# A two-layer decoder kernel: order of early loads, a product split over chunks, and passes moved between engines

## Chip, cores and metric

The kernel runs on one core of one Trainium2 chip. Its time is the device time of one execution in microseconds, as a median over runs. A second execution is recorded by the hardware profiler, and all durations below come from that record. The core has a matrix engine (TensorE, PE), three engines for elementwise work (VectorE or DVE, ScalarE or ACT, GpSimd or POOL) and a queue engine (SyncE or SP). DMA transfers are issued from the instruction streams of SP, ACT and POOL. PEld is the load of a stationary operand, which overlaps with PE.

## What is computed

Two layers work on `x` of shape (2, 512, 1024) with a context of shape (2, 1024, 1024), all in float32:

```python
x = x + fake_quant(layernorm(x)) @ fake_quant(ctx)            # layer 0, first part
x = x + layer_0_ffn(layernorm(x))                             # W, b, and routed low-rank terms
x = x + attention(layernorm(x), ctx, ctx, mask, wq, wk, wv, wo)   # layer 1: 32 heads, 8 key heads, rope
x = x + layer_1_ffn(layernorm(x))                             # W_up and a gated low-rank term

def fake_quant(x, scale, zp):
    q = clip(round(x / scale + zp), 0, 255)
    return (q - zp) * scale

# routing in layer_0_ffn: one softmax for each batch from the mean of some rows
q = x[:, 179:-1, :].mean(axis=1)
routing = softmax(q @ router_W.T + router_b)                  # 8 experts
```

The gate of the last part takes the best of four experts for each token.

## The kernel before

**Products.** Each large product is done by a scheme with seven block products instead of eight. A left matrix and a right matrix are cut into quarters, sums of quarters are made (`left_steps`, `right_steps`: four sums each), and seven products of sums are accumulated in 128x512 PSUM banks (`seven`, in the order 1, 2, 6, 7, 5, 4, 3). Products 1 and 2 need only raw quarters, the others need sums. A generator yields after each block product. `pair(a, b)` alternates two such generators for two products each and then runs them one after the other; `weave` advances a side generator between the yields of a main one. There are four PSUM tiles with the tag "b", each one bank, and two of the tag "wide", each two banks. SBUF tiles come from four groups of buffers: u8 (14), u4 (17), u2 (10) and small (16).

**Order.** TensorE's order is the order of the program text everywhere. VectorE's and ScalarE's order is the program's in two places, inside the blocks that say so: the first stage, and all of attention up to its last steps, where GpSimd's is too. Elsewhere a planner, which works from modelled costs when the kernel is built, orders VectorE, ScalarE, GpSimd and the queues. SP's queue is always ordered by the planner. Each engine and each queue then runs strictly in that order, so one that waits holds back all behind it.

**Start.** The first stage computes keys of batch 0 in rotated form (`keys`, `rope_steps`). L1043 to L1046 load the first key weight quarter on SP and the first context quarter on ScalarE's queue in four chunks each; L1047 to L1062 load the rest in order of need. Eight small constants (quantizer scales and zero points, router bias and weights, gate bias and weights) are loaded by GpSimd's queue at the top (L119, L139 to L146), and VectorE derives six more from them (L123 to L133).

**Layer 0, first part.** `quantized_product` is a side generator. It loads eight 128x1024 rows of the context for each batch, quantizes them with three VectorE passes each (L194, L197, L198), does the same with four normalized rows of `x`, turns those by TensorE (L431, copied out by L156) and multiplies. `copy_out`, L284 (first copy in `seven`), L216 and L217 (the halves of the rope rotation) and L434 run on ScalarE. Meanwhile the main stream does the remaining keys and then the values. `quad_weights` (L370) issues four weight loads on SP and makes their sums; it is called after each stage's `weave`.

**Router.** `routed` makes the mean row (`qm`) on VectorE, then eight f32 products of 128x128 with 128x8 on TensorE (L630), and the softmax.

**Queries and the seam into attention.** `queries` makes query heads four at a time for q = 0 to 7. A rope is done in two steps: the two ScalarE copies (L216, L217), and then three elementwise passes (L219 on VectorE, L222 and L223 on the engine given). For q = 7 the second step is put into the list `later`, on GpSimd; `rotate` in attention runs it. Attention runs from step n = -2 on; head n+2 is new, n+1 is in the middle, n is old. Each step has three phases: scores of the new head (L768, with the mask added by L782 on VectorE); a tree of maxima (L790 to L796) with products of other stages in between, whose number for q = 7 is in `extra`; then maximum and sum over partitions (L732, L734), written to a row in DRAM (L741) and read back broadcast (L747), the copy of the maximum into a PSUM bank (`place_maximum`, L810), two halves of the exponential (L814 on VectorE, L817 on ScalarE, sums L820 to L825 on GpSimd), and the product with the values (`attend`, L831, copied out by L839). L842 normalizes on GpSimd in the next step.

**Gates.** Near the end, `gated` is advanced by hooks at (step, phase): products with the gate weights (L967, copied out by L975), transposes (L981), a chain of small VectorE passes (L982 to L996), transposes back (L1005). `projection` (`seven_onto`, first copy L320) and `linear` are the products around it.

Of the kernel before, what the change touches and what calls it, by code (L numbers as in the profile page):

```python
# [18 lines left out]
P = 128  # L19
# [20 lines left out]
def decoder_kernel(  # L40
# [67 lines left out]
    eps_t = const.tile([P, 1], F32, name="eps_t")  # L108
    nc.gpsimd.memset(eps_t, EPS)
    prefer = const.tile([P, E1], F32, name="prefer")  # L110
# [6 lines left out]
    for name, ap in qparams.items():  # L117
        t = const.tile([P, 1], F32, name=f"qp_{name}")
        nc.gpsimd.dma_start(t, ap.partition_broadcast(P))  # L119
        qp[name] = t  # L120
    for side in ("x1", "x2"):
        t = const.tile([P, 1], F32, name=f"qp_inv_{side}")
        nc.vector.reciprocal(t, qp[f"{side}_scale"])  # L123
        qp[f"{side}_inv"] = t
# [3 lines left out]
    for c_t, side in ((c_x1, "x1"), (c_x2, "x2")):  # L128
        nc.vector.tensor_scalar(c_t, qp[f"{side}_zp"], -1.0, QMID, ALU.mult, ALU.add)
    kc2 = const.tile([P, 1], F32, name="kc2")  # L130
    nc.vector.tensor_scalar_mul(kc2, c_x2, float(D))
    s12 = const.tile([P, 1], F32, name="s12")
    nc.vector.tensor_tensor(s12, qp["x1_scale"], qp["x2_scale"], ALU.mult)  # L133
# [5 lines left out]
    nc.gpsimd.dma_start(rb_t, rb0.partition_broadcast(P))  # L139
    eb_t = const.tile([P, E1], F32, name="eb_t")  # L140
    nc.gpsimd.dma_start(eb_t, ebias.partition_broadcast(P))
    r0_t = const.tile([P, NC, E0], F32, name="r0_t")
    nc.gpsimd.dma_start(r0_t, r0T.rearrange("(c p) e -> p c e", p=P))
    NGA = E1 + E1 * R1
    ga_t = const.tile([P, NC, NGA], F32, name="ga_t")
    nc.gpsimd.dma_start(ga_t, gaT.rearrange("(c p) e -> p c e", p=P))  # L146
# [45 lines left out]
    def quantized(dst, src, side):  # L192

        nc.vector.tensor_scalar(  # L194
            src, src, qp[f"{side}_inv"], qp[f"{side}_zp"], ALU.mult, ALU.add
        )
        nc.vector.tensor_scalar(src, src, 0.0, QMAX, ALU.max, ALU.min)  # L197
        nc.vector.tensor_scalar(dst, src, RND, RND + QMID, ALU.add, ALU.subtract)  # L198
# [71 lines left out]
    def seven(product, emit):  # L270
# [5 lines left out]
        for i in (1, 2, 6, 7, 5, 4, 3):  # L276
            first = {2: 1, 4: 7, 3: 5}.get(i, i)
            if i == first:
                banks[i] = ps_b()
            acc = banks[first]  # L280
            product(i, acc, i == first)
# [82 lines left out]
    def quad_weights(dram, q):  # L364

        raw = []
        for mh in range(2):
            for ch in range(2):
                w = u4([P, 4, 256])
                nc.sync.dma_start(w, dram[q, mh, ch])  # L370
                raw.append(w)
        return quad_sums(raw)
# [109 lines left out]
    def keys(b, q, ctx_ops, w):  # L482
        def group(m):
            def product(i, acc, start):
                accumulate(
                    acc,
                    [(w[i - 1][:, c, ts(m, P)], ctx_ops[i - 1][:, c, :]) for c in range(4)],
                    start,
                )

            def emit(i, j, src):
                dst = u2([P, HALF]) if (i, j) == (0, 0) else src
                rope(dst, src, j, 1.0)
                nc.sync.dma_start(kT_d[b][4 * q + 2 * i + m][:, ts(j, HALF)], dst)

            return seven(product, emit)

        return group(0), group(1)
# [110 lines left out]
    def routed(b, quarters, a_t, b_t, result):  # L609
# [15 lines left out]
        nc.vector.tensor_scalar_mul(qm[:, 0, :], qm[:, 0, :], 1.0 / (Q_END - Q_START))  # L625
        yield
        yield
        racc = ps_b()
        for c in range(NC):
            nc.tensor.matmul(  # L630
                racc[:, :E0],
                qm[:, 0, c : c + 1].to_broadcast([P, P]),
                r0_t[:, c, :],
                start=(c == 0),
                stop=(c == NC - 1),
            )
# [31 lines left out]
    def queries(q, h_ops, w, later=None):  # L668

        def head(m):  # L670
# [7 lines left out]
            def finish(i, j, src):  # L678
                dst = u2([P, HALF]) if (i, j) == (0, 0) else src
                eng = nc.vector if later is None else nc.gpsimd  # L680
# [175 lines left out]
    def attention(extra):  # L856
# [28 lines left out]
        for n in range(-2, total + GRP + 1):  # L885
# [36 lines left out]
            for _ in range(extra.pop(n, 0)):  # L922
                for _ in range(2):
                    next(tree, None)
                next(extra["products"])
            if n == GRP:
# [5 lines left out]
            if mid:  # L932
                mid.place_maximum()
# [109 lines left out]
    for c in range(4):  # L1043
        cs = slice(c, c + 1)
# [31 lines left out]
    with tc.manual_schedule(engines={mybir.EngineType.DVE, mybir.EngineType.Activation}):  # L1076
# [3 lines left out]
        advance(lefts, 2)  # L1080
        for g in first[0]:
# [17 lines left out]

    side = layer_0()  # L1100
    for b in range(B):
# [5 lines left out]
        for i, stage in enumerate((keys, keys, values, values)):  # L1107
# [57 lines left out]
    early = [head for q in range(2) for head in queries(q, h_ops, w[q])]  # L1165
# [9 lines left out]
    for q in range(NH // 4):  # L1175
        heads = (
            early[2 * q : 2 * q + 2]
            if q < 2
            else queries(q, h_ops, w, later if q == NH // 4 - 1 else None)
        )  # L1180
# [3 lines left out]
        if q < NH // 4 - 1:  # L1184
            for _ in main:
                pass
# [5 lines left out]
    extra = {-2: 3, -1: 3, 0: 2, 1: 2, 2: 2, 3: 1, 4: 1}  # L1192
# [40 lines left out]
    for i in range(2):  # L1233
# [11 lines left out]
    hooks[(62, 1)] = [lambda: advance(last["gates"], 3)]  # L1245
    hooks[(62, 2)] = [
        lambda: fetch_weight(7, 0, 1),
        lambda: fetch_weight(3, 1, 1),
    ]
    with tc.manual_schedule(  # L1250
# [6 lines left out]
        for i in range(3 * (B * NH + 2)):  # L1257
# [4 lines left out]
            if (n - 2, phase) == (63, 1):  # L1262
                zT = next(last["gates"])
# [6 lines left out]
                advance(main, 2)  # L1270

# [123 lines left out]
```

## Time and profile before

| what | us |
|---|---|
| median of 3 runs (lowest to highest) | 2451.58 (2450.2 to 2452.53) |
| the profiled execution | 2450.07 |
| its span, first to last instruction | 2448.3 |
| TensorE busy in the span | 2412.5 |
| first key product waits, last chunk used from | 13.74 |
| first value product begins | 114.26 |
| attention begins, first scores | 929.97 |
| last matmuls | from 2416.90 |

The span is what the instructions of the kernel cover; the execution has 1.8 us more around it. In all views, times count from the first instruction. A row of a timeline has the start, the time that the merged instructions took, engine, line, operation, the tile written and those read, the shape, how many they are, and in brackets the idle time before them with what ended it. The page also cuts the span into 40 equal slices; these two lines give the busy share of TensorE and of the DMA engines in each, in tenths:

```profile
PE   8999999999999999999999999999999999999999
...
DMA  5537133013796221244323323442433343233501
```

TensorE is full nearly everywhere. The DMA engines are full only around 650 to 750 us, and half used at the start.

### The profile page before, as it was taken

To read this page: it belongs to the slowest core of one execution; us is meant where nothing else is said; L and a number is where in the kernel's file an instruction comes from. 1 tells how busy PE (TensorE), PEld (TensorE's weight loads), DVE (VectorE), ACT (ScalarE), POOL (GpSimd) and SP (SyncE) were. 2 spreads that over 40 slices of the span, in tenths; PEclk is the share of its full clock that TensorE was granted. 3 is DMA by queue.
4 is the path that set the end of the run, shared out by engine and by line. 5 is a ranking of instruction groups with operands and counts; after the bars stand their busy time and mean duration, and the time that the engine had idled before them with its cause. 6 is when DMAs were issued, how large, how long until landed. Compare 5 with 4: busy or idle time off the path is not lost.

```text
span 2448.3 us, 19583 instructions
## 1 busy us (share of the span) xinstructions
PE 2412.5 (99%) x6792; PEld 1195.8 (49%) x6800; DVE 1841.1 (75%) x1994; ACT 530.8 (22%) x623; POOL 1031.3 (42%) x550
## 2 busy tenths in 40 slices
PE   8999999999999999999999999999999999999999
PEld 3477458654444443444444444444444444444444
DVE  4949774345876556898888888888898998888653
ACT  1210221011222222322222222222222222222210
POOL 0000010210000001677676767667776767677621
PEclk9999999999999999999999999999999999999999
DMA  5537133013796221244323323442433343233501
GB/s 182 181 105 273 69 134 108 26 60 116 274 330 216 78 91 56 77 156 111 81 83 107 114 65 90 142 145 79 125 116 79 94 125 112 66 90 108 172 9 60
DMA packets 149010, 288.01 MB, mean 118 GB/s; under 512 B 29424, under 2 KB 47360, under 8 KB 146608
## 3 DMA queue, kind: packets, MB, share of 16 engines
q1 hardware_dynamic: 108080, 244.35, 29.9%
q10 hardware_dynamic: 40400, 41.70, 6.9%
q8 instruction: 54, 0.88, 0.2%
q0 software_dynamic: 432, 0.71, 0.1%
q14 instruction: 44, 0.36, 0.1%
HBM read 223.54 MB, written 63.18 MB: 117 GB/s over the span
## 4 chain that ended last, share of the span: by engine, by line
PE 60%; DVE 6%; POOL 2%; issue 1%; DMA 1%; ACT 1%; ACTq 0%; SPq 0%; DVEq 0%; POOLq 0%
PE b L355 26%; PE wide L768 16%; PE b L831 15%; PE wide L732 2%; DVE u L814 2%; DMA u<-in_wo_dram 1%; DVE u L782 1%; POOL u L823 0%; POOL u L824 0%; DVE small L734 0%; DVE u L792 0%; DVE u L794 0%; ACT u L817 0%; POOL u L825 0%; DVE u L328 0%
## 5 line engine op out<-in xcount | busy, mean ns | idle before, releaser
L355 PE MATMUL b<-u,u 128*128 128x512 f32 (+1 forms) x3616 | 1394.2, 542 | 21.3 <-DMA u<-in_ctxT_in_dram 7.6
L355 PEld LDWEIGHTS b<-u,u 128*128 128x128 f32 x3616 | 684.6, 191 | 695.9 <-issue 612.8
L768 PE MATMUL wide<-u,u 128*128 128x512 f32 x1024 | 454.8, 595 | 7.3 <-DVE u L782 6.4
L831 PE MATMUL b<-u,u 128*128 128x512 f32 x1024 | 460.3, 592 | 0.0
L782 DVE TENSOR_TENSOR u<-wide,u 128x1024 f32<-128x1024 f32 x256 | 312.8, 1224 | 130.3 <-PE wide L768 129.9
L817 ACT ACTIVATE u<-u 128x2048 f32<-128x2048 f32 x128 | 244.7, 1912 | 655.8 <-DVE u L814 593.9
L768 PEld LDWEIGHTS wide<-u,u 128*128 128x128 f32 x1024 | 193.4, 190 | 257.3 <-issue 177.9
L814 DVE TENSOR_TENSOR u<-u,b 128x2048 f32<-128x2048 f32 x128 | 290.2, 2268 | 0.0
L820 POOL TENSOR_TENSOR u<-u 128x1024 f32<-128x1024 f32 x64 | 151.5, 2367 | 317.5 <-ACT u L817 310.1
L831 PEld LDWEIGHTS b<-u,u 128*128 128x128 f32 x1024 | 186.2, 192 | 184.6 <-issue 184.6
L310 POOL TENSOR_TENSOR u<-u,u 128x512 f32<-128x512 f32 x120 | 188.5, 1597 | 175.4 <-DVE u L322 153.2
L328 DVE TENSOR_TENSOR u<-u,b 128x512 f32<-128x512 f32 x200 | 135.8, 680 | 126.0 <-PE b L355 125.9
L222 POOL TENSOR_TENSOR u<-u,sin_t 128x512 f32<-128x512 f32 x8 | 11.6, 1456 | 402.7 <-ACT u L217 402.7
L823 POOL TENSOR_TENSOR u<-u,u 128x1024 f32<-128x1024 f32 x64 | 150.7, 2354 | 36.4 <-ACT u L817 36.0
L824 POOL TENSOR_TENSOR u<-u,u 128x1024 f32<-128x1024 f32 x64 | 150.8, 2356 | 5.0
L842 POOL TENSOR_TENSOR u<-u,u 128x512 f32<-128x512 f32 x64 | 119.9, 1873 | 10.0 <-DMA u<-row 10.0
L216 ACT ACTIVATE u<-u 64x512 f32<-64x512 f32 x72 | 45.2, 628 | 356.3 <-DVE u L293 177.6
L790 DVE TENSOR_TENSOR u<-u 128x1024 f32<-128x1024 f32 x64 | 115.8, 1810 | 0.0
L732 PEld LDWEIGHTS wide<-ident,u 128*128 128x128 f32 x512 | 79.6, 203 | 63.9 <-issue 55.0
L612 POOL TENSOR_TENSOR u<-u,u 128x1024 f32<-128x1024 f32 x8 | 20.2, 2529 | 214.9 <-DVE u L168 111.6
L792 DVE TENSOR_TENSOR u<-u,u 128x1024 f32<-128x1024 f32 x64 | 105.4, 1646 | 0.2
L825 POOL TENSOR_TENSOR u<-u 128x512 f32<-128x512 f32 x64 | 101.0, 1578 | 5.0
(135 smaller groups left out, 1614.3 us busy)
## 6 DMA issues: line engine op xcount, KB each, us to landing
u<-row ACTq DMA_DIRECT2D x128, 256.0 KB, 3.7
u<-wo SPq DMA_DIRECT2D x64, 512.0 KB, 4.0
u<-in_wo_dram SPq DMA_DIRECT2D x48, 512.0 KB, 4.5
u<-in_wq_dram SPq DMA_DIRECT2D x32, 512.0 KB, 4.2
q<-u SPq DMA_DIRECT2D x64, 256.0 KB, 2.4
u<-in_wo_dram SPq DMA_DIRECT2D x16, 1024.0 KB, 8.2
wo<-u SPq DMA_DIRECT2D x32, 512.0 KB, 4.2
u<-q SPq DMA_DIRECT2D x64, 256.0 KB, 4.2
```

Of the source, the lines that this page charges most:

```text
L310: nc.gpsimd.tensor_tensor(c, c, what, ALU.add)
L328: nc.vector.tensor_tensor(c, c, acc, ALU.add)
L355: nc.tensor.matmul(acc, lhsT, rhs, start=start and k == 0, stop=k == len(pairs) - 1, skip_group_check=True,)
L732: nc.tensor.transpose(tr[:, t, :], src[:, t, :], ident)
L768: nc.tensor.matmul(sc[:, ts(n, HALF)], self.kT[:, ts(2 * j + n, P)], self.qT, start=True, stop=True,)
L782: nc.vector.tensor_tensor(self.e[j // 2][:, js, :], sc.rearrange("p (k q) -> p k q", k=2), mask[j], ALU.add)
L814: nc.vector.tensor_tensor(e, e, self.nmf.unsqueeze(1).to_broadcast([P, 4, S]), ALU.add)
L817: nc.scalar.activation(e, e, AF.Exp)
L820: nc.gpsimd.tensor_tensor(d, e[:, 0:2, :], e[:, 2:4, :], ALU.add)
L823: nc.gpsimd.tensor_tensor(d, d, e[:, 0:2, :], ALU.add)
L824: nc.gpsimd.tensor_tensor(d, d, e[:, 2:4, :], ALU.add)
L831: nc.tensor.matmul(self.acc, self.v[:, k, :], self.e[j][:, k % 4, :], start=(k == 0), stop=(k == NKT - 1),)
```

## The change

Eight edits, in the order of the program:

1. The eight small loads leave GpSimd's queue and come on SP behind the last weight of the first stage. The constants made from them come after the first stage.
2. The first pass of the quantizer (`x * inv + zp`) runs on ScalarE instead of VectorE, 24 passes in all.
3. The first quarter products of keys 0 and 1 are computed together, chunk by chunk, into two banks (`begun`) that `seven` then takes as product 1. The loads come in three chunks, of one, one and two 128-row blocks. Twenty 128x128 bf16 products on a tile of ones come ahead of them.
4. The raw value weights for the first value stage are requested before the weave of the second key stage instead of after it; the sums of them stay after it.
5. The router's eight products become an elementwise product and a sum on VectorE, and one product with ones.
6. `queries` takes its rope engine as an argument; q = 6 also defers its second rope step by one yield, and its last one goes into attention. The steps -2 and -1 of attention do 2 and 4 products instead of 3 and 3, and in step -1 the maximum and both exponentials stand between these products.
7. In every later step the read of the sum's row (`old.den`) comes after the second exponential instead of before the new maximum.
8. The third step of the gates comes after attention of its step, and the last one after the first two products of `linear`.

```diff
@@ constants
-    eps_t = const.tile([P, 1], F32, name="eps_t")
+    eps_one = const.tile([P, 2], F32, name="eps_one")
+    eps_t, one_t = eps_one[:, 0:1], eps_one[:, 1:2]
     nc.gpsimd.memset(eps_t, EPS)
+    nc.gpsimd.memset(one_t, 1.0)
...
-    for name, ap in qparams.items():
-        t = const.tile([P, 1], F32, name=f"qp_{name}")
-        nc.gpsimd.dma_start(t, ap.partition_broadcast(P))
-        qp[name] = t
-    for side in ("x1", "x2"):
-        t = const.tile([P, 1], F32, name=f"qp_inv_{side}")
-        nc.vector.reciprocal(t, qp[f"{side}_scale"])
-        qp[f"{side}_inv"] = t
+    for name in list(qparams) + ["x1_inv", "x2_inv"]:
+        qp[name] = const.tile([P, 1], F32, name=f"qp_{name}")
...
@@ def quantized(dst, src, side):
-        nc.vector.tensor_scalar(
-            src, src, qp[f"{side}_inv"], qp[f"{side}_zp"], ALU.mult, ALU.add
+        nc.scalar.activation(
+            src, src, AF.Identity, bias=qp[f"{side}_zp"], scale=qp[f"{side}_inv"]
         )
@@ def seven(product, emit, begun=None):
-                banks[i] = ps_b()
+                banks[i] = begun if begun is not None and i == 1 else ps_b()
             acc = banks[first]
-            product(i, acc, i == first)
+            if begun is None or i > 1:
+                product(i, acc, i == first)
@@ def quad_weights(dram, q):
+        return quad_sums(raw_weights(dram, q))
+
+    def raw_weights(dram, q):
         raw = []
...
-        return quad_sums(raw)
+        return raw
@@ def routed(b, quarters, a_t, b_t, result):
+        weighted, each = u2([P, E0, NC]), small([P, E0])
+        nc.vector.tensor_tensor(
+            weighted,
+            r0_t.rearrange("p c e -> p e c"),
+            qm[:, 0, :].unsqueeze(1).to_broadcast([P, E0, NC]),
+            ALU.mult,
+        )
+        nc.vector.tensor_reduce(each, weighted, AX.X, ALU.add)
         yield
         yield
         racc = ps_b()
-        for c in range(NC):
-            nc.tensor.matmul(
-                racc[:, :E0],
-                qm[:, 0, c : c + 1].to_broadcast([P, P]),
-                r0_t[:, c, :],
-                start=(c == 0),
-                stop=(c == NC - 1),
-            )
+        nc.tensor.matmul(
+            racc[:, :E0], one_t.to_broadcast([P, P]), each, start=True, stop=True
+        )
@@ def queries(q, h_ops, w, eng, later=None):
-                eng = nc.vector if later is None else nc.gpsimd
@@ attention, phase 2
-            for _ in range(extra.pop(n, 0)):
+            for i in range(extra.pop(n, 0)):
                 for _ in range(2):
                     next(tree, None)
                 next(extra["products"])
+
+                if mid and not old and i == 1:
+                    mid.place_maximum()
+                    mid.exponential(0)
+                if mid and not old and i == 2:
+                    mid.exponential(1)
@@ attention, phase 3
-            if mid:
+            if mid and old:
                 mid.place_maximum()
...
                 old.attend(0)
-            if mid:
-                mid.exponential(0)
-            if old:
-                old.den = from_row(old.den)
+                if mid:
+                    mid.exponential(0)
                 if new:
                     new.turn_maximum()
-            if mid:
-                mid.exponential(1)
+                if mid:
+                    mid.exponential(1)
+                old.den = from_row(old.den)
@@ first loads
-    for c in range(4):
-        cs = slice(c, c + 1)
+    for c in range(3):
+        cs = slice(c, c + 1 + c // 2)
         nc.sync.dma_start(wk_raw[0][0][:, cs, :], wk[0, 0, 0][:, cs, :])
         load_context(nc.scalar, 0, 0, cs)
...
+    for name, ap in qparams.items():
+        nc.sync.dma_start(qp[name], ap.partition_broadcast(P))
+    nc.sync.dma_start(rb_t, rb0.partition_broadcast(P))
+    nc.sync.dma_start(eb_t, ebias.partition_broadcast(P))
+    nc.sync.dma_start(r0_t, r0T.rearrange("(c p) e -> p c e", p=P))
+    nc.sync.dma_start(ga_t, gaT.rearrange("(c p) e -> p c e", p=P))
...
-    first = [keys(0, q, ctx_ops, w[q]) for q in range(2)]
+    begun = [ps_b() for _ in range(2)]
+
+    for i in range(20):
+        nc.tensor.matmul(begun[0][:, :P], ones_b, ones_b, start=True, stop=True)
+    first = [keys(0, 0, ctx_ops, w[0], begun), keys(0, 1, ctx_ops, w[1])]
...
+        for c in range(4):
+            for m in range(2):
+                nc.tensor.matmul(
+                    begun[m],
+                    wk_raw[0][0][:, c, ts(m, P)],
+                    ctx_raw[0][:, c, :],
+                    start=(c == 0),
+                    stop=(c == 3),
+                )
         for g in first[0]:
             next(g)
@@ stages
                 main = chain(*first[1])
+                raw = raw_weights(wv, 0)
+                weave(main, side, 2)
+                w = quad_sums(raw)
             else:
                 main = pair(*stage(b, i % 2, ctx_ops, w))
-            weave(main, side, 2)
-            if i < 3:
-                w = quad_weights((wk, wv)[(i + 1) // 2], (i + 1) % 2)
+                weave(main, side, 2)
+                if i < 3:
+                    w = quad_weights((wk, wv)[(i + 1) // 2], (i + 1) % 2)
@@ queries and the seam
+        heads = early[2 * q : 2 * q + 2]
+        if q > 1:
+            last_two = q >= NH // 4 - 2
+            heads = queries(
+                q, h_ops, w, (nc.vector, nc.gpsimd)[q == NH // 4 - 1], later if last_two else None
+            )
...
-            for _ in main:
-                pass
+            for i, _ in enumerate(main):
+
+                if i < 13:
+                    for rotation in later:
+                        next(rotation, None)
+                    later.clear()
...
-    extra = {-2: 3, -1: 3, 0: 2, 1: 2, 2: 2, 3: 1, 4: 1}
+    extra = {-2: 2, -1: 4, 0: 2, 1: 2, 2: 2, 3: 1, 4: 1}
@@ gates
-    hooks[(62, 1)] = [lambda: advance(last["gates"], 3)]
+    hooks[(62, 1)] = [lambda: advance(last["gates"], 2)]
     hooks[(62, 2)] = [
+        lambda: next(last["gates"]),
...
             if (n - 2, phase) == (63, 1):
-                zT = next(last["gates"])
...
                 advance(main, 2)
+                zT = next(last["gates"])
```

More of the change, by code (lines that the diff above doesn't have):

```diff
@@ L116, in decoder_kernel @@
     qp = {}
-    for name, ap in qparams.items():
-        t = const.tile([P, 1], F32, name=f"qp_{name}")
-        nc.gpsimd.dma_start(t, ap.partition_broadcast(P))
-        qp[name] = t
-    for side in ("x1", "x2"):
-        t = const.tile([P, 1], F32, name=f"qp_inv_{side}")
-        nc.vector.reciprocal(t, qp[f"{side}_scale"])
-        qp[f"{side}_inv"] = t
+    for name in list(qparams) + ["x1_inv", "x2_inv"]:
+        qp[name] = const.tile([P, 1], F32, name=f"qp_{name}")
     c_x1 = const.tile([P, 1], F32, name="c_x1")
     c_x2 = const.tile([P, 1], F32, name="c_x2")
-    for c_t, side in ((c_x1, "x1"), (c_x2, "x2")):
-        nc.vector.tensor_scalar(c_t, qp[f"{side}_zp"], -1.0, QMID, ALU.mult, ALU.add)
     kc2 = const.tile([P, 1], F32, name="kc2")
-    nc.vector.tensor_scalar_mul(kc2, c_x2, float(D))
     s12 = const.tile([P, 1], F32, name="s12")
-    nc.vector.tensor_tensor(s12, qp["x1_scale"], qp["x2_scale"], ALU.mult)
     ident_b = const.tile([P, P], BF16, name="ident_b")
@@ L138, in decoder_kernel @@
     rb_t = const.tile([P, E0], F32, name="rb_t")
-    nc.gpsimd.dma_start(rb_t, rb0.partition_broadcast(P))
     eb_t = const.tile([P, E1], F32, name="eb_t")
-    nc.gpsimd.dma_start(eb_t, ebias.partition_broadcast(P))
     r0_t = const.tile([P, NC, E0], F32, name="r0_t")
-    nc.gpsimd.dma_start(r0_t, r0T.rearrange("(c p) e -> p c e", p=P))
     NGA = E1 + E1 * R1
     ga_t = const.tile([P, NC, NGA], F32, name="ga_t")
-    nc.gpsimd.dma_start(ga_t, gaT.rearrange("(c p) e -> p c e", p=P))
     cos_t = [const.tile([P, HALF], F32, name="cos_t"), None]
@@ L268, in right_steps, with seven @@
         yield [b11, b21, b22, t4, t1, t2, b12]
-    def seven(product, emit):
+    def seven(product, emit, begun=None):
         banks = {}
@@ L479, in quantized_product, with keys @@
             yield
-    def keys(b, q, ctx_ops, w):
+    def keys(b, q, ctx_ops, w, begun=(None, None)):
         def group(m):
@@ L494, in emit @@
                 nc.sync.dma_start(kT_d[b][4 * q + 2 * i + m][:, ts(j, HALF)], dst)
-            return seven(product, emit)
+            return seven(product, emit, begun[m])
         return group(0), group(1)
@@ L665, in routed, with queries @@
         yield
-    def queries(q, h_ops, w, later=None):
+    def queries(q, h_ops, w, eng, later=None):
         def head(m):
@@ L1098, in decoder_kernel @@
         load_rows(0, nc.scalar)
+    for side in ("x1", "x2"):
+        nc.vector.reciprocal(qp[f"{side}_inv"], qp[f"{side}_scale"])
+    for c_t, side in ((c_x1, "x1"), (c_x2, "x2")):
+        nc.vector.tensor_scalar(c_t, qp[f"{side}_zp"], -1.0, QMID, ALU.mult, ALU.add)
+    nc.vector.tensor_scalar_mul(kc2, c_x2, float(D))
+    nc.vector.tensor_tensor(s12, qp["x1_scale"], qp["x2_scale"], ALU.mult)
     side = layer_0()
@@ L1164, in decoder_kernel @@
     h_ops = [hb[0][0], hb[0][1]] + [None] * 5
-    early = [head for q in range(2) for head in queries(q, h_ops, w[q])]
+    early = [head for q in range(2) for head in queries(q, h_ops, w[q], nc.vector)]
     for _ in range(2):
@@ L1175, in decoder_kernel @@
     for q in range(NH // 4):
[L1176 to L1180, printed above, removed]
+        heads = early[2 * q : 2 * q + 2]
[4 more added lines that the diff above has]
+            )
         main = chain(*heads) if q < 2 else pair(*heads)
```

## Prediction, written before the change was run

> **What bounds the kernel now.** I read the busy times first, then the waits of TensorE, then the stretches around each wait, because the busy line leaves only one question open:
>
> ```profile
> PE 2412.5 (99%) x6792; PEld 1195.8 (49%) x6800; DVE 1841.1 (75%) x1994; ACT 530.8 (22%) x623; POOL 1031.3 (42%) x550
> ```
>
> TensorE works for 2412.5 of 2448.3 us. So the end moves only by what is taken out of TensorE's own stream, or by the 36 us in which it stands still or runs slowly. The view of its waits (total us, times, longest) says where:
>
> ```profile
> PE b L355 <- DMA u<-in_ctxT_in_dram: 7.6, 4, 3.9
> PE wide L768 <- DVE u L782: 6.4, 6, 3.6
> PE b L355 <- DMA u<-in_wv_dram: 4.1, 1, 4.1
> PE b L355 <- ACT u L320: 2.5, 1, 2.5
> PE b L355 <- ACT u L284: 1.8, 2, 1.6
> ```
>
> The timeline of TensorE at these places (start, length, line, count, idle before) also shows what a wait costs afterwards:
>
> ```profile
> 3.88 2.08 PE L355 MATMUL b<-u,u 128*128 128x512 f32 x2 [3.88 <-DMA u<-in_ctxT_in_dram]
> 6.16 2.05 PE L355 MATMUL b<-u,u 128*128 128x512 f32 x2 [0.20 <-DMA u<-in_ctxT_in_dram]
> 10.46 2.04 PE L355 MATMUL b<-u,u 128*128 128x512 f32 x2 [2.26 <-DMA u<-in_ctxT_in_dram]
> 13.74 56.50 PE L355 MATMUL b<-u,u 128*128 128x512 f32 x125 [1.24 <-DMA u<-in_ctxT_in_dram]
> ...
> 114.26 12.31 PE L355 MATMUL b<-u,u 128*128 128x256 f32 x48 [4.10 <-DMA u<-in_wv_dram]
> 126.41 0.61 PE L431 MATMUL wide<-ident_b,u 128*128 128x128 bf16 x8
> 128.61 7.17 PE L355 MATMUL b<-u,u 128*128 128x256 f32 x32 [1.59 <-ACT u L284]
> ...
> 406.50 1.85 PE L630 MATMUL b<-r_t,small 128*128 128x8 f32 x16
> ...
> 935.05 3.70 PE L768 MATMUL wide<-u,u 128*128 128x512 f32 x8 [1.40 <-DVE u L782]
> 974.19 5.40 PE L768 MATMUL wide<-u,u 128*128 128x512 f32 x8 [3.60 <-DVE u L782]
> ...
> 2293.35 1.99 PE L355 MATMUL b<-u,u 128*128 128x512 f32 x4 [2.48 <-ACT u L320]
> ```
>
> Two kinds of loss are in these rows: the gap itself, and a slow stretch behind a long one. Eight instructions take 3.70 us after a gap of 1.40, but 5.40 after one of 3.60. Four take 1.99 after 2.48, near the usual 1.88. At the start they come 0.855 us apart until 19.0 us and 0.429 from there.
>
> **The change, part by part.** One f32 matmul is two instructions of 0.429 us, so a product of four pairs is 3.43 us of TensorE.
>
> *Start, -5.1.* Before, head 0's product 1 (eight instructions) waits for four chunks one after the other. Head 1's product 1 follows, and product 2 begins at 20.73, the tenth instruction after 13.74. After, both heads use each chunk as it lands. When the third and last load lands (chunks 2 and 3 together), eight instructions are left, 3.4 us at full speed. Product 2 needs the second context tile, whose first half was issued on ScalarE's queue at 4.23 and landed 13.1 us later, at 17.36. What can bring it forward: from 3.88 to 13.74 the DMA engines were 0.81 busy, so 1.9 us are unused, and the eight small loads of GpSimd's queue took 5.2% of the engines in the first 30 us, 1.6 us. With both the tile lands at 13.9, with neither at 17.36; I take the middle, 15.6. The gain is 20.73 - 15.6 = 5.1. Bounds: 7.4 if only TensorE limits (16 instructions from 3.88, six slow: 3.88 + 5.1 + 4.3 = 13.3), and 0.2 if the last chunk lands at 13.7 as before and eight run slowly (13.7 + 6.8 = 20.5). The gain lasts if VectorE's sums come in time. Product 6 began at 41.2 and would begin at 36.1; its operand from L248 was there at 33.6, so 2.5 us of cover are left. Without it, a larger gain waits for L250, done at 38.8.
>
> *The 20 bf16 products on ones* run from about 1.1, when ones_b is set, before the first chunk at 3.88. Eight bf16 products of 128 columns (L431) took 0.61, so 20 take 1.5, or 3.1 at half speed, ending at 4.2: -0 to +0.3, taken as 0. The slow stretch ended 5.3 us after work became steady at 13.74, so here I expect full speed by about 8. [...]
>
> *The eight small loads* go from GpSimd's queue to SP's, behind the last key weight, issued at 20.82. An issue there takes 0.33 to 0.43, so 3.2 us in all, while SP's next was a key store at 35.53. That idle time hides them; without it the stores come 3 us late. Their first user was VectorE's L194 at 77.4. Six VectorE constants of 0.15 move from idle time at 9 to 13 into a busy stretch: 0.9 us, paid out of the scales that leave.
>
> *Value weights, -5.9.* The four loads were issued at 110.38 and from 114.17, behind key stores that wait for VectorE. After, they stand ahead of stage 2's stores. The wait of 4.10 goes, and so does the slow stretch: 48 instructions took 12.31, while 32 at full speed take 7.07, so 48 take 10.5, and 1.8 are saved. Next in line is the copy L284 (1.59 at 128.61), which stood behind L156 on ScalarE; I leave it in. Bounds: 0 (see the rivals) to 7.5 with that wait gone too. What SP now does later are the context rows for the quantizer, and those share 17 buffers with the four weights.
>
> *Quantizer scales, 0.* 24 VectorE passes of 0.81 (19.5 us) become 24 of ScalarE; nearest row: L434, 1.06 for the same 128x1024. VectorE was 42.5 of 46 busy from 64 to 110, but TensorE never waited there. ScalarE was busy 9.3 of 46 and has the room. Behind each new pass stand the rope copies L216 and L217 and the bank copy L284. [...] Bounds: the waits of TensorE from 195 to 930 sum to 4.2, and the planner's new order may remove or double them: -4.2 to +4.2.
>
> *Router, -3.0.* Sixteen instructions hold TensorE from 406.50 to 408.20, and two are left (0.21): 1.5 less, twice. VectorE's product and sum (nearest: L996 at 0.29 and L114 at 0.27) have two yields of cover; without it they cost 0.6 each time.
>
> *Seam into attention, -4.1.* Before: waits of 0.63, 1.40 and 3.60 and a slow 1.7 (5.40 against 3.70), 7.3 in all. Count from the first scores, 0. The last rope of q=6 leaves VectorE's path, so L782 starts at 1.9 instead of 3.8 and the 1.40 goes. That rope now stands ahead of head 1's L782s: three passes of 0.69 where one stood, a new wait of 0.7. In the next step four products run. Queued behind L810 are L814 (2.28), then L288, then L814. L810 itself follows b2's copies, done at about 30.1, so L814 ends at 33.1 and L288 at 33.7. Five accumulator banks are wanted where four exist: a and b until their ropes, the maximum, product 6, and product 7. Product 7 is ready at 32.1 and gets a bank at 33.75: a new wait of 1.65. The scores after it wait 0.3 for L782 behind L734 and two L219. What remains is 0.63 + 0.7 + 1.65 + 0.3 = 3.3, a saving of 4.05. Bounds: -7.3 (no new wait) to +1.6. The latter has product 7 take the maximum's bank after the second L814 (2.3 more) and the query load behind a store one product later (3.4 more).
>
> *Order in attention, 0.* The read of the sum's row moves behind the second exponential. GpSimd's L842 waits for it: on head steps near 1325 it landed at 1328.4 and L842 began at 1336.3, so 2 to 3 us later is covered by L823 to L825; without that cover L842 is 2 us late. TensorE's waits from 981 to 2268 total 4.8 (1287.0 less 1282.2): -4.8 to +4.8.
>
> *Gates, -3.0.* The wait of 0.48 before L981 goes, since attention of head 62 is put ahead of it. Its chain of VectorE passes (2280.12 to 2284.0) no longer precedes L734 and both L814, so they, L817 and L320 come some 4 us sooner and the 2.48 goes. zT now follows two products of 3.43, cover for that chain. Bounds: -3.0 to 0.
>
> Sum: -5.1 - 5.9 - 3.0 - 4.1 - 3.0 = -21.1. The profiled execution took 2450.07 with a span of 2448.3, so I expect a span of 2427.2 and 2429.0 for that execution. The median shown is 1.5 above it: 2451.58 - 21.1 = **2430.5**.
>
> **Rivals.**
> *Cold start:* if the last load comes too long after the second chunk's work ends, somewhere between the gaps of 2.48 (no slow rows behind it) and 3.60 (slow rows), the eight left run slowly, 8 x 0.43 = 3.4 later: 2433.9. For it: the gap I expect, from 8.1 to some 11 or 12, is about 3. Against: a little more DMA speed closes it. Chance 0.15. [...]
> *Weights early, quantizer late:* four weights hold four of 17 buffers; context rows wait, and the transposes L431 wait for them. Price: the 5.9, and one more round of load 6.3 and passes 1.06 + 0.69 + 0.69 = 8.7, of which VectorE's 9 saved scales (7.3) cover all but 1.4: 2430.5 + 5.9 + 1.4 = 2437.8. The same 5.9 is lost if the planner leaves the loads behind the stores. For it: VectorE was full from 77 to 120. Chance 0.15.
> *Seam moves its waits only:* 2434.6 to 2436.2, with no gain or a loss of 1.6. Chance 0.1.
> *Other side, ScalarE in order:* each scale stands ahead of a copy out of an accumulator that TensorE waits for, as L156 did at 127.06 for 1.59. Price 24 x (1.06 + 0.12 hand-over; VectorE waited 1.39 for two passes of 0.63) = 28.6: 2459.1, slower. It decides from 0.88 us for each scale on. Against: only about a third lie beside rope copies. Chance 0.1.
>
> **Numbers.** Forecast 0.5, its own range 2423 to 2437. A measurement of this kernel tells a change from none at about 0.2%, 4.9 us. All cases but the last are faster by that much unless several losses meet, which leaves 0.06 for no change; slower, with unforeseen waits, 0.11; faster 0.83. The range for 8 in 10: 2419 (the forecast, with half of the best ends: 2.3 + 1.6 + 4.2 + 3.2) to 2445 (two rivals together and a few new small waits).
>
> **What would show it.** Product 2 at about 15.6 and rows 0.43 apart by 8; no wait on the value weights and full speed behind; two instructions at the router; at the seam a wait near 1.7 on an accumulator bank in place of 3.60 on L782; no wait at L320 near the end. I am wrong if new waits on ScalarE (L216, L284) stand between 60 and 270, or if L431 waits for quantized rows.

## The result, and the profile after

The kernel after takes 2438.96 us (median of 6 runs, 2437.86 to 2440.54), the kernel before beside it 2451.58 (6 runs, 2448.6 to 2454.22). The ratio is 0.995, with a 95% interval of 0.9937 to 0.9963. The forecast was 2430.5, with a range of 2419 to 2445. The span of the profiled execution went from 2448.3 to 2437.1.

The busy line of the page after, and the waits of TensorE (total us, times, longest):

```profile
PE 2408.2 (99%) x6792; PEld 1195.4 (49%) x6792; DVE 1826.9 (75%) x1974; ACT 556.1 (23%) x647; POOL 1025.0 (42%) x543
```

```profile
PE b L345 <- DVE u L281: 11.9, 5, 5.9
PE b L345 <- ACT u L274: 2.9, 1, 2.9
...
PE b L345 <- DVE u L278: 1.3, 1, 1.3
```

The three entries that headed the list before, on context chunks, on the mask's sum and on the value weights, are gone or down to 1.5 at most. New at the head is L281: VectorE's sum out of the bank of product 7 in `seven` (the lines moved: the new scale is L182, `seven`'s copy L274, its sums L278 to L290, the mask's sum L777). The timeline of TensorE shows where (start, length, line, count, idle before):

```profile
1.06 2.31 PE L1078 MATMUL b<-ones_b 128*128 128x128 bf16 x20 [1.06 <-DVE ones_b L129]
3.87 8.96 PE L1095 MATMUL b<-u,u 128*128 128x512 f32 x16 [0.49 <-DMA u<-in_ctxT_in_dram]
12.67 31.15 PE L345 MATMUL b<-u,u 128*128 128x512 f32 x72
44.73 51.77 PE L345 MATMUL b<-u,u 128*128 128x512 f32 x120 [0.92 <-DVE u L281]
102.43 19.17 PE L345 MATMUL b<-u,u 128*128 128x512 f32 x64 [5.94 <-DVE u L281]
...
124.95 8.86 PE L345 MATMUL b<-u,u 128*128 128x256 f32 x32 [2.90 <-ACT u L274]
...
227.62 19.16 PE L345 MATMUL b<-u,u 128*128 128x256 f32 x56 [2.57 <-DVE u L281]
...
962.25 3.70 PE L345 MATMUL b<-u,u 128*128 128x512 f32 x8 [1.25 <-DVE u L278]
...
2278.65 12.18 PE L345 MATMUL b<-u,u 128*128 128x512 f32 x28
```

Product 2 begins at 12.67 instead of 20.73. The first value stage no longer waits for its weights. But three places between 44 and 236 us became worse: 5.94 at 102.43, 2.90 at 124.95 (1.59 before) and 2.57 at 227.62, with slow rows behind them: behind the second of these gaps 32 instructions take 8.86, where they took 7.17 before.

In the next table TensorE's stream is cut at the same instructions in every profile, so each number is the length of a piece of the same work with its waits. The names of the other columns are explained with the experiments. "Keys" runs from product 2 to the last key product; "values, first 48" takes in the wait for the weights.

| piece, us | before | after | e1 | e2 | e3 | e4 | e5 | e6 | e9 |
|---|---|---|---|---|---|---|---|---|---|
| start, to product 2 | 20.73 | 12.67 | 12.45 | 13.89 | 13.76 | 20.71 | 13.70 | 12.70 | 14.06 |
| keys of batch 0 | 89.43 | 98.42 | 98.62 | 89.96 | 90.13 | 89.27 | 89.39 | 91.39 | 94.20 |
| values, first 48 | 16.25 | 10.36 | 10.36 | 10.36 | 16.87 | 10.36 | 10.36 | 10.36 | 10.36 |
| transposes and wait for the copy | 2.20 | 3.51 | 4.73 | 4.90 | 2.20 | 3.88 | 4.20 | 2.20 | 3.51 |
| quantized product and values between | 67.17 | 68.86 | 68.86 | 68.86 | 67.17 | 68.86 | 68.86 | 67.17 | 67.17 |
| last values of batch 0 | 37.99 | 42.51 | 37.99 | 42.02 | 37.99 | 42.21 | 37.99 | 37.99 | 42.14 |

From before to after the sum of these is +2.6, although the start gave 8.1 and the weights 5.9: 16.5 were given back. What lies behind 236 us gained 13.8, where 10.1 was forecast (router, seam and gates; the order in attention was put at 0).

### The profile page after: what moved, and what is told of

Its sections match the earlier page's. It is cut to its first block, busy times and chain, and to the rows that moved or that the text cites. A ratio compares the mean times of both kernels' runs of the same rounds, so it can differ in the third digit from the quotient of the medians.

```text
span 2437.1 us, 19528 instructions
## 1 busy us (share of the span) xinstructions
PE 2408.2 (99%) x6792; PEld 1195.4 (49%) x6792; DVE 1826.9 (75%) x1974; ACT 556.1 (23%) x647; POOL 1025.0 (42%) x543
## 4 chain that ended last, share of the span: by engine, by line
PE 54%; DVE 5%; issue 1%; POOL 0%; ACT 0%; POOLq 0%; ACTq 0%; DVEq 0%
PE b L345 19%; PE wide L763 16%; PE b L826 16%; PE wide L727 2%; DVE u L809 1%; DVE u L789 0%; DVE u L787 0%; DVE u L318 0%; DVE small L729 0%; DVE u L777 0%; PE b L967 0%; PE wide L192 0%; DVE u L791 0%; DVE small L151 0%; POOL u L818 0%
## 5 line engine op out<-in xcount | busy, mean ns | idle before, releaser
L777 DVE TENSOR_TENSOR u<-wide,u 128x1024 f32<-128x1024 f32 x256 | 312.8, 1224 | 125.2 <-PE wide L763 125.0
L300 POOL TENSOR_TENSOR u<-u,u 128x512 f32<-128x512 f32 x120 | 184.4, 1563 | 170.7 <-DVE u L312 134.9
L837 POOL TENSOR_TENSOR u<-u,u 128x512 f32<-128x512 f32 x64 | 115.4, 1804 | 18.0 <-DMA u<-row 18.0
```

Of the source, the lines that this page charges most:

```text
L300: nc.gpsimd.tensor_tensor(c, c, what, ALU.add)
L777: nc.vector.tensor_tensor(self.e[j // 2][:, js, :], sc.rearrange("p (k q) -> p k q", k=2), mask[j], ALU.add)
```

## The experiments

Three theories for the 16.5. A: the scales on ScalarE, each a hand-over in order. B: the value weights requested early, which make the quantizer's rows late. C: the earlier start alone, which puts TensorE ahead of loads that did not move. The first four kernels take the two edits apart. Ratios are to the kernel before, run beside each group: its median was 2450.01 for e1 to e4, 2449.8 for e5 to e8 and 2450.24 for e9 to e12. Across groups the ratios compare better than the times.

**e1: the scales back on VectorE, weights early.**

```diff
-        nc.scalar.activation(
-            src, src, AF.Identity, bias=qp[f"{side}_zp"], scale=qp[f"{side}_inv"]
+        nc.vector.tensor_scalar(
+            src, src, qp[f"{side}_inv"], qp[f"{side}_zp"], ALU.mult, ALU.add
         )
```

> The kernel after, with the 24 quantizer scales back on VectorE and nothing else undone. Three theories of the 16.5 us that TensorE lost between 50 and 235 us (8.98 by the end of the keys stage, 3.0 at the copy behind it, 4.51 before 236). Theory A, the scales on ScalarE: VectorE stands in order behind its hand-overs (it waited 3.22 us for one L182 at 85.8), so the sums of the banks come late. It expects the waits of 5.94 at 102.4 and 2.57 at 227.6 gone, and 2438.96 - 16.5 = 2422.5, at most 2428. Theory B, the value weights early: they hold 4 of 17 buffers and the rows for the quantizer come late, whoever scales them. It expects 2438 to 2446, with the wait near 102 still there. Theory C, the earlier start: TensorE is 8 us ahead of loads that did not move. It expects the wait near 102 at about its old length and 2437 to 2441.

Measured 2434.12 (ratio to before 0.9934, 0.9917 to 0.995). The last piece of the table went back to 37.99, as A says; the keys stayed at 98.62, as B says. The time lies outside what each of the three theories gave. The wait for the copy grew instead of going, from 2.90 to 4.12, with slow rows behind it:

```profile
126.16 8.86 PE L345 MATMUL b<-u,u 128*128 128x256 f32 x32 [4.12 <-ACT u L274]
```

No scale stands ahead of the copy in this kernel. A step of the layer norm does (L163), which waits on ScalarE 1.75 for VectorE's L152 and ends at 125.4.

**e2: the weights late, scales on ScalarE.**

```diff
-                raw = raw_weights(wv, 0)
                 weave(main, side, 2)
+                raw = raw_weights(wv, 0)
                 w = quad_sums(raw)
```

> The kernel after, with the four loads of the first value weights back behind the second keys product; scales stay on ScalarE. The wait on the value weights comes back in any case (4.1 and a slow stretch of 1.8 in the kernel before, 5.9). Theory A (scales): the waits near 102 and 228 stay, so 2438.96 + 5.9 = 2444.9. Theory B (early weights): the wait near 102 (5.94, with slow rows 8.98 in all) goes: 2438.96 - 9.0 + 5.9 = 2435.9. Theory C (earlier start): the wait near 102 stays, 2443 to 2446.

Measured 2433.09 (0.9931, 0.9916 to 0.9946). The keys went back to 89.96, 8.5 less, as B says. What no theory had: the wait for the weights did not come back (10.36). The planner gave SP another order: three of the four weights stand behind 13 of the 16 key stores and go from 94.83 on. In the kernel before one stands behind 14 stores and three behind 15, and these go from 114.17 on.

**e3: both undone.**

> The kernel after, with both undone: scales on VectorE, value weights late. Theory A: 2422.5 + 5.9 = 2428.4. Theory B: the same as with the weights alone undone, 2436, or less by what the other undoing gives. Theory C: a wait near 102 stays though neither edit is there, 2443 to 2446.

Measured 2432.04 (0.9926, 0.9911 to 0.994). Keys 90.13, so C falls: the start of this kernel is nearly as early (13.76), and the long wait near 100 is gone. Now the wait for the weights is back (16.87), and three of them stand behind 15 stores again, from 107.92 on.

**e4: the kernel before with nothing but the scales on ScalarE.**

> The kernel before, with only the 24 scales put on ScalarE. Theory A: slower than before by what the three new waits cost, 2451.6 + 9 to 16 = 2461 to 2468, with a wait on VectorE's sums near 100. Theory B and theory C: the scales alone cost nothing, 2450 to 2453.

Measured 2450.74 (1.0005, 0.9995 to 1.0014): no change in all, as B and C say, but made of parts that cancel. The first 48 values gain 5.9, the copy and the rows behind it lose 1.7 and 1.7, the last values 4.2; the pieces leave a loss of 1.5, less than the interval can tell. So the two edits each remove the same wait for the value weights. Done together the second removes nothing more, and its cost stays. e4 has e2's order too: three weights behind 13 stores, from 99.93 on.

*Why early weights cost 8.5.* SP's timeline, first of the kernel after, then of e2 (L487 stores keys, L363 loads value weights, L414 loads a context row):

```profile
57.18 0.67 SPq L363 DMA_DIRECT2D u<-in_wv_dram  x1
66.33 0.32 SPq L487 DMA_DIRECT2D kT<-u  x1
66.70 0.92 SPq L363 DMA_DIRECT2D u<-in_wv_dram  x2
71.47 0.33 SPq L487 DMA_DIRECT2D kT<-u  x1
71.89 0.38 SPq L363 DMA_DIRECT2D u<-in_wv_dram  x1
72.37 0.41 SPq L414 DMA_DIRECT2D u<-in_ctx_in_dram  x1
```

```profile
57.48 0.68 SPq L414 DMA_DIRECT2D u<-in_ctx_in_dram  x1
...
66.75 0.92 SPq L414 DMA_DIRECT2D u<-in_ctx_in_dram  x2
...
71.94 0.87 SPq L414 DMA_DIRECT2D u<-in_ctx_in_dram  x2
```

The weights, which TensorE first uses at 111, take exactly the four places of the first four rows, at 57, 67, 67 and 72. The first row is requested 15 us later; in e2 ScalarE uses it from 69.5 on. Between the places SP stands before key stores that wait for VectorE's last rope pass, L211 (from 50 to 80 us 21.9 in five waits, the longest 8.4). Why only one or two loads go between two stores is not shown: it can be the planner's order, or the group of 17 buffers that rows and weights share. VectorE then runs dry, and gets the passes in one heap. The stretch from 80 to 95 us (length, VectorE busy, instructions, TensorE's clock, DMA share, GB/s), after and then e2:

```profile
80.00:95.00 15.00, 8.36 (x15) 1.00 0.85 330
```

```profile
80.00:95.00 15.00, 13.06 (x23) 1.00 0.53 210
```

VectorE's timeline after shows the dry spell and what the heap does to the bank's sum:

```profile
85.83 0.69 DVE L185 TENSOR_SCALAR u<-u 128x1024 f32<-128x1024 f32 x1 [3.22 <-ACT u L182]
...
100.50 0.68 DVE L278 TENSOR_TENSOR u<-u,b 128x512 f32<-128x512 f32 x1
101.10 0.69 DVE L186 TENSOR_SCALAR u<-u 128x1024 bf16<-128x1024 f32 x1
101.70 0.68 DVE L281 TENSOR_TENSOR u<-u,b 128x512 f32<-128x512 f32 x1
```

L281 empties the bank for which TensorE waits until 102.43, and it stands in a fixed order behind the late passes. With scales on VectorE (e1) the same 8.5 are lost, in three waits of 0.91, 3.31 and 0.75 and slow rows.

**e9: two weights early, two late.** A dose, to test the places.

```diff
-                raw = raw_weights(wv, 0)
+                raw = raw_weights(wv, 0, (0,))
                 weave(main, side, 2)
-                w = quad_sums(raw)
+                w = quad_sums(raw + raw_weights(wv, 0, (1,)))
```

> The kernel after with two of the four value weights early and two behind the second keys product. Four early cost 8.4 us between product 2 and the end of the keys stage (98.4 us against 90.0 with all four late), and took, on SP's queue, the places of the first four context rows at 57, 67, 67 and 72 us. Theory of the places: each early weight puts the rows one place back, so two cost about half, 4.2: 2434.7, and rows begin at the third place, near 67. Rival, that any early weight makes the planner put VectorE's passes ahead of the bank sums: the full 8.4 stays, 2439. Rival, slack for two: 2431.

Measured 2434.62 (0.9934, 0.992 to 0.9949). The first row is requested at 67.81, the third place; the keys take 94.20, 4.2 more than e2 (a wait of 2.50, and 1.7 of slow rows). The theory of the places holds, and so does its number: half the weights, half the cost.

**e5: e2 with the 12 scales of batch 1 on VectorE.** The calls pass `b == 0` for `on_act`.

```diff
+        if on_act:
             nc.scalar.activation(
                 src, src, AF.Identity, bias=qp[f"{side}_zp"], scale=qp[f"{side}_inv"]
             )
+        else:
+            nc.vector.tensor_scalar(
+                src, src, qp[f"{side}_inv"], qp[f"{side}_zp"], ALU.mult, ALU.add
+            )
```

> The kernel after with the value weights late (the run that did so took 2433.1), and with the 12 scales of batch 1 back on VectorE; the 12 of batch 0 stay on ScalarE. It asks what the wait near 221 to 228 is, which shows with scales on ScalarE and not without. Theory D: VectorE has less to do, so in its order a sum of the key weights (L233) now stands ahead of the bank's sum L281 and waits 4.62 us for a load that lands at 219.32. With batch 1's scales on VectorE the order turns back, the wait (2.08, with slow rows 4.2 in all) goes: 2429. Theory E, the hand-over from ScalarE itself, expects the same here only for batch 1's scales, and the waits before 125 unchanged at 0.3 and 4.3 in both. If the wait stays, both fall: 2433.

Measured 2429.35 (0.9916, 0.9899 to 0.9932); the last values take 37.99 (42.02 in e2). VectorE's timeline after, and of e5 (whose lines are five further: L238 is L233, L286 is L281):

```profile
225.74 1.23 DVE L233 TENSOR_TENSOR u<-u,u 128x1024 f32<-128x1024 f32 x1 [5.12 <-DMA u<-in_wk_dram]
226.88 0.68 DVE L281 TENSOR_TENSOR u<-u,b 128x512 f32<-128x512 f32 x1
```

```profile
215.74 0.67 DVE L286 TENSOR_TENSOR u<-u,b 128x512 f32<-128x512 f32 x1
...
219.74 1.21 DVE L238 TENSOR_TENSOR u<-u,u 128x1024 f32<-128x1024 f32 x1
```

After, VectorE stands 5.12 us before a weight sum whose load is late, with the bank's sum behind it. In e5 the bank's sum comes first. So the wait at 227.62 is no hand-over from ScalarE: VectorE has less to do, the planner moved a weight sum ahead, and the load did not come sooner.

**e6: e2 with only the 8 scales of batch 0's context rows on ScalarE.** The edit is shown against e5.

```diff
-            quantized(l1, h, "x1", b == 0)
+            quantized(l1, h, "x1", False)
```

> The same with only the 8 scales of batch 0's context rows on ScalarE; those of the x rows (4 for each batch) and all of batch 1 are on VectorE. It asks what makes the copy out of the bank (L274) late: 4.29 us with all scales on ScalarE against 1.59 with none. Theory: on ScalarE the copy stands behind L182 of an x row, which itself waits for L156 on VectorE behind four sums of 1.14 us. Expected: the copy's wait back at about 1.6, and the slow rows behind it (1.7) gone, 4.4 less than with all of batch 0's on ScalarE, and still no wait on the value weights: 2424.5. Rival: those 4 passes fill VectorE again and the value weights are late as before: 2428 to 2431.

Measured 2424.23 (0.99, 0.9885 to 0.9915), the lowest median; the interval lies below that of the kernel after, and overlaps those of e5 and of e10 to e12. Its profile is of its slowest execution, 2429.10 (the other three: 2422.91 to 2424.45). ScalarE's timeline after, then of e6 (L274 and L279 are the copy out of the bank, L144 the copy of the transposes):

```profile
122.09 1.01 ACT L144 COPY u<-wide 128x1024 bf16<-128x1024 bf16 x1 [1.69 <-PE wide L424]
...
123.00 1.24 ACT L182 ACTIVATE u<-u,qp_x_zp,qp_x_inv 128x1024 f32<-128x1024 f32 x1
...
124.33 0.57 ACT L274 COPY u<-b 128x512 f32<-128x512 f32 x1
```

```profile
115.10 1.01 ACT L144 COPY u<-wide 128x1024 bf16<-128x1024 bf16 x1 [4.43 <-PE wide L429]
...
116.00 0.59 ACT L279 COPY u<-b 128x512 f32<-128x512 f32 x1
```

Without the scale of an `x` row between them the copy's wait is 1.59 again (4.29 in e2, 2.90 after) and no slow rows follow. With the weights late, theory A is right here; in the kernel after, the same place takes 1.3 and 1.7 of the 16.5. But e1 shows that with the weights early the scales are not the whole cause: without them the wait is 4.12. The 8 scales left are enough to keep the value weights in time.

**e7 and e8: the start.** Both are e2 with one thing undone: the 20 bf16 products left out (e7), or the eight small loads at the top on GpSimd's queue again (e8).

```diff
-    for i in range(20):
-        nc.tensor.matmul(begun[0][:, :P], ones_b, ones_b, start=True, stop=True)
```

> The kernel after with the value weights late, without the 20 bf16 products on ones. If they bring the clock up before the first chunk lands, product 2 begins later without them: the first rows run at half speed, 16 products of 0.43 at most 6 us, and I expect 3 us of it at the start (2436). If the loads alone set the start, product 2 begins within 0.3 us of 13.9 and the time is 2433.

```diff
-        nc.sync.dma_start(qp[name], ap.partition_broadcast(P))
+        nc.gpsimd.dma_start(qp[name], ap.partition_broadcast(P))
...
```

> The kernel after with the value weights late, and the small loads of constants back at the front on GpSimd's queue. It asks how much of the earlier start is theirs: the second context tile landed at 11.9 to 12.1 after and at 17.36 before. If they took the DMA engines' time as I counted it (1.6 us of 16 engines), product 2 begins 1 to 2 us later than 13.9 and the time is 2434 to 2435; if each delays the large loads more than its bytes, 3 to 5 us later, 2436 to 2438.

e7: 2431.38 (0.9924, 0.9909 to 0.9939), not to be told from e2's 2433.09. Product 2 begins at 13.51, inside the 12.45 to 14.06 of the kernels that have them. My 3 us were wrong: the 16 instructions ahead of it take 9.82 from 3.85 on, and 10.10 from 3.96 on in e2 with the 20 products, so the loads set the start. In the kernel after, the first row at 0.43 is that of 7.16. e8: 2437.73 (0.9949, 0.9934 to 0.9964), product 2 at 15.96, 2.1 later than in e2; its keys take 92.14, 2.2 more than e2's. So the start alone lost about what was expected from the loads' own time, 1 to 2, but the whole time is that of the other case, 2436 to 2438. What the DMA engines moved in the first 24 us, in 40 slices, in the kernel after and then in e8:

```profile
GB/s 0 0 7 171 336 350 224 171 278 369 403 416 420 410 403 403 389 396 413 403 416 393 399 389 399 406 406 372 393 389 396 399 399 399 389 389 389 386 386 399
```

```profile
GB/s 0 0 0 154 295 348 230 249 307 222 120 247 389 325 349 236 187 249 142 311 291 234 281 337 372 375 413 413 386 403 406 403 379 389 389 396 389 416 396 382
```

From the tenth slice on, where the small loads are under way, the rate falls to 120 to 390 and stays low for some 9 us. In those 24 us e8 moves 7.09 MB, after 8.31, and e2, from which e8 differs in these loads alone, 8.36. SP's own requests come later too (a key weight load at 15.84 that e2 has at 11.52); which of the two holds up the other is not shown.

**e10, e11, e12: e6 with the later edits undone one by one.** Of e11 and e12 only the first lines are shown.

```diff
@@ e10
-                if new:
-                    new.turn_maximum()
-                if mid:
-                    mid.exponential(1)
                 old.den = from_row(old.den)
+                if new:
+                    new.turn_maximum()
+                if mid:
+                    mid.exponential(1)
@@ e11
-    extra = {-2: 2, -1: 4, 0: 2, 1: 2, 2: 2, 3: 1, 4: 1}
+    extra = {-2: 3, -1: 3, 0: 2, 1: 2, 2: 2, 3: 1, 4: 1}
...
@@ e12
-    hooks[(62, 1)] = [lambda: advance(last["gates"], 2)]
+    hooks[(62, 1)] = [lambda: advance(last["gates"], 3)]
...
```

> The best kernel so far (value weights late, 8 scales on ScalarE; 2424.2), with the read of the sum's row put back ahead of the second exponential. From 1000 to 2256 us the change gained 1.5 us that I had put at 0. If this move made it, 1.5 come back between those places: 2425.7, and waits of 0.2 to 0.9 on L727 near 1921 and 2008 as before. If not, 2424.2 and the same waits as with the move.

> The best kernel so far with the seam undone: products 3 and 3 instead of 2 and 4, the exponentials of the first head behind the products, the last rope of q=6 in VectorE's stream. The seam gained 4.98 between 928 and 995 us where I had put 4.1. If that is all it does, 5.0 come back there: 2429.2, with waits of about 1.4 and 3.6 on the mask's sum L777 and slow rows (5.4 for 8). If the gain is paid elsewhere, less.

> The best kernel so far with the order of the gates undone near the end. The change gained 3.62 between 2264 and 2310 us where I had put 3.0. Expected: the waits of 0.48 at L981 and 2.5 on L320's copy come back, and 3.0 to 3.6 with them: 2427.2 to 2427.8.

The ratios of all three overlap that of e6, so only places can tell them from it. e10: 2426.61 (0.9901, 0.9887 to 0.9916). Attention takes 1283.0 between the fourth scores and the gate products, 1279.1 in e6; waits of 0.39, 0.46 and 0.59 on GpSimd's L825 came at 1649, 1901 and 1988, and one of 0.79 at 1627. But e4, whose attention is that of the kernel before, takes 1278.7 for the same piece and the kernel before itself 1280.8. So what the order is worth stays open, between nothing and some 4 us.

e11 (with the exponentials and the last rope of q=6 put back too): 2427.37 (0.991, 0.9893 to 0.9926). From the first to the fourth scores it takes 64.17, e6 59.16: the 5.0 are there, with the waits as expected:

```profile
917.16 3.70 PE L768 MATMUL wide<-u,u 128*128 128x512 f32 x8 [1.61 <-DVE u L782]
...
956.31 5.23 PE L768 MATMUL wide<-u,u 128*128 128x512 f32 x8 [3.60 <-DVE u L782]
```

e12: 2428.22 (0.9907, 0.9893 to 0.9922). Waits of 0.48 on the gates' copy and 1.72 on the projection's first copy came, not 2.5, and by place 2.6 came back, from the gate products to the last product with the values (27.04 against 24.41).

## Why the prediction came out as it did

The range of 2419 to 2445 held the time and the direction was right, but the time is 8.5 above the forecast and 2 above the forecast's own range, which ended at 2437. By the profiled spans 11.2 of the 21.1 came: a surplus of about 6.6 in several steps and a loss of 16.5 in three. That so much of one cancelled the other is luck; the mechanism of the largest loss was in a rival with a chance of 0.15. Of the prediction's own signs of being wrong one came true: the wait on ScalarE's bank copy (L284, now L274), between 60 and 270, grew from 1.59 to 2.90. The transposes wait for no quantized row.

- *Start, -5.1: measured -8.1.* The mechanism was right, the term too small. The join of the two heads and the three loads give 4.8 by themselves (20.73 to 15.96 in e8, which has the bf16 products too). The move of the small loads gives another 1.9 to 3.5 (15.96 to 14.06 or 12.45). I had priced it by the time of its own packets, 1.6, and taken the middle between having and not having the better DMA rate. The bound of 7.4 took six slow rows; with the bf16 products there were four.
- *The 20 bf16 products, 0:* right for the time (e7).
- *The eight small loads on SP's queue, 0:* right. But the issues are spread from 17.3 to 28.4 instead of taking 3.2, and the first key store is not at 35.53 but at 30.73, as the rope's last pass L211 ends at 30.70; 2.4 us of cover were left.
- *Value weights, -5.9: the wait and the slow rows went, -5.9; the step failed beside it.* I wrote that the context rows and the four weights share buffers, and left the price to a rival. That rival had the cause: the weights take the rows' places. The keys cost 8.98 more here, of which e2 puts 8.5 to this edit. The rival's 7.3 and its time of 2437.8 were near, but by chance: its price takes the 5.9 of the wait as lost, and that gain came. It had the wrong waiter: not the transposes, but L281 on a full, ordered VectorE. Nor did I see that the moved scales alone remove the same wait (e4), so that this edit had nothing left to earn.
- *Copy L284, "I leave it in": +3.0.* The scale of an `x` row came between the two copies, 1.3 longer, and slow rows followed, 1.7 more. Taking the scale away gives both back when the weights are late (e6), but not when they are early (e1).
- *Quantizer scales, 0, bounds of 4.2 on either side from 195 us on: +4.5.* I named the planner's new order as the risk and took the middle. The wait at 227.62 is that order (e5). The rival of 28.6 us from ScalarE in order (28.3 by the terms it shows) is far off: e4 shows no loss in all, and 4.2 of the 7.6 that it gives back is no hand-over. The row for a scale was 1.06; L182 takes 1.24.
- *Router, -3.0: -3.1.* Right; two instructions are left.
- *Seam, -4.1: -5.0.* Right in kind, e11 gives the same by place. The wait on the bank for product 7 that I forecast at 1.65 is 1.25 at 962.25, and the one ahead of head 1's scores 0.41 instead of 0.7.
- *Order in attention, 0: -1.5,* not settled (e10).
- *Gates, -3.0: -3.6.* Right in kind, 0.6 beyond its bound; no wait is left there. The undoing alone brings back 2.6 by place (e12).
- *Cold start:* did not come; no gap over 0.5 is left ahead of product 2.

One stretch limits how finely totals can be compared. From 606 to 929 us, with the same program, profiles of these kernels differ between 321.7 and 328.3 us, with waits of 0.3 to 2.0 on L281 and L283. That is why e1, e2 and e3 are told apart by place and not by their totals, and why e11's total gives 3.1 where the place gives 5.0. e6's profile has the longest of these stretches.

## What to carry to other kernels

Before a load is moved forward, look for the load whose place in the queue it takes: four weights needed at 111 us cost 8.5 us because they went ahead of rows used from 69 on. Two edits that cure one wait must not be added up: here each alone gained the same 5.9 (e1, e4). When an ordered engine gets lighter, a waiting instruction can move ahead of one that empties a bank (after, VectorE stood 5.12 us before a weight sum, with L281 behind it); check what stands behind every wait on a load.

## What was not expected of the hardware

**Slow rows.** They do not follow from the length of the gap alone. The same gap of 2.90 before the same work is followed by slow rows in the kernel after and by none in e9. Stretches of 2 us (length, TensorE busy, instructions, granted clock, DMA share, GB/s), after and then e9:

```profile
125.00:127.00 2.00, 2.00 (x8) 0.83 1.05 410
127.00:129.00 2.00, 2.00 (x6) 0.50 0.72 175
129.00:131.00 2.00, 2.00 (x9) 0.81 0.94 318
```

```profile
122.00:124.00 2.00, 1.87 (x9) 1.00 1.03 396
124.00:126.00 2.00, 2.00 (x11) 1.00 0.86 262
```

After, the clock falls to 0.50 some 1.4 us behind the restart at 124.95, for 7 to 8 instructions of 0.43, some 3.4 us, and the cost is 1.7. In e7 a gap of 1.98 (before 219.98) was enough, and the clock fell some 0.3 us behind it; in the kernel before one of 2.48 was not. The first two stretches of e7:

```profile
219.00:221.00 2.00, 1.02 (x3) 0.82 0.00 0
221.00:223.00 2.00, 2.00 (x6) 0.50 0.00 0
```

From 20 us on, the gaps of 3.27 (e4), 3.31 and 4.12 (e1), 3.60 (before, e11), 3.99 (e3), 4.10 (before), 4.29 (e2) and 5.94 (after) had slow rows behind them, and those of 1.59 to 1.81 in the kernels before and after had none. In between, both occur: the gaps of 1.98 (e7), 2.08 (e2), 2.27 (e4), 2.50 (e9), 2.57 and 2.90 (after) had them, those of 2.48 (before) and 2.90 (e9) had not. The stretch can be longer too: in e1, behind a gap of 3.31 that ends at 86.25, the granted clock from 80 to 95 us is 0.77 in the mean, from which I estimate 6.9 us at 0.50 (15 x 0.23 / 0.50). What else decides is not shown.

**Small loads.** Eight loads of 0.19 MB in 288 packets, whose own time was 7.0% of the engines in the first 24 us (1.7 us), lowered what all moved in that time by 1.2 MB; at the 346 GB/s of the kernel after that is an estimated 3.5 us. What delays the large loads is not shown.
